# Attention with heads of 96 taken by pairs of tiles instead of by heads, with shared key chunks, and the last linear layer put inside it for one half of the rows

## The chip, the cores and the metric

The kernel runs on one core of one Trainium2 chip. The metric is the device time of one execution in microseconds (us); before the change the median of three runs is 1843.64 us (1840.32 to 1844.16). Six names are used for what works in a core: PE is the tensor engine (matrix products; "PEld" its weight loads), DVE the vector engine, ACT the scalar engine, POOL the GpSimd engine, SP the engine whose queue issues the loads and stores (DMAs), and PSUM the memory of eight banks into which PE writes.

## The reference

Four decoder layers, each a cross-attention and a feed-forward step, on 16 sequences of 64 tokens with width 512. Everything is float32. The change concerns the last layer, and moves some memory of the third. What matters of it, shortened:

```python
# layer 3, attention: 16 query heads, 4 key/value heads, head width 96
hidden = concatenate([context, latents], axis=1)          # 64 + 64 rows per sequence
q = (latents @ Wq.T).reshape(b, 64, 16, 96)
k = (hidden @ Wk.T).reshape(b, 128, 4, 96)
v = (hidden @ Wv.T).reshape(b, 128, 4, 96)
scores = einsum('bkgqd,bksd->bkgqs', q, k) / sqrt(96)     # 4 query heads share a key head
out = einsum('bkgqs,bksd->bkgqd', softmax(scores), v)
x = x + out.reshape(b, 64, 16 * 96) @ Wo.T
# layer 3, feed-forward: a 3-bit weight, unpacked in groups of 32
w = weight_q3 / 7.0 * (x_max - x_min) + x_min
x = x + layernorm(x) @ w.T + bias
```

Each step works on the layernorm of x, and adds to x.

## The kernel before, in words

**Tiles.** The 1024 rows are eight tiles of 128 rows (two sequences each); x lies in on-chip memory as `x[0]` to `x[7]`. `kvT` holds, transposed, the normed rows and the context rows of every tile.

**Lanes.** Two streams of work share the engines, lane a (`main`) and lane b (`side`). Lane b does the first layer, lane a the attention of the second; then lane b does layers 1f, 2 and 3 for tiles 0 to 3 and lane a the same for tiles 4 to 7. Each lane has four PSUM banks of its own (`Lane.bank`, tag `ps_a` or `ps_b`, `bufs=4`).

**Order.** Each layer is a generator that yields a planner's cost after each step, and `merged` runs lane b's steps until their costs have caught up with lane a's. PE executes in exactly the order in which these steps are written out (`manual_schedule` names PE alone). The other engines and the SP queue get an order from a planner that lays out the instructions when their inputs are ready. `ticks(units, steps)` (L184) is a software pipeline: in tick n, each step of the list, in order, works on unit n minus its lag.

**Slots.** A tile taken from a pool with a tag gets one of that tag's `bufs` pieces of memory, and keeps it until its last reader is done; the next tile of the tag waits for a free one. This holds for PSUM banks too.

**`packed_attention`** (L1153) first computes the values of the eight sequences of the lane (`v_all`, L1177), while `Normed.need` keeps the layernorms and their transposes (`xn`, an own tag with two slots) a little ahead. Then its units run head by head: (head h, tile pair t), eight per lane. Per unit: `keys` (L1209; four chunks of the contraction, 96 outputs wide, 512 columns), `scores` of the unit before, `queries` (L1224; three output chunks of 128, 256 columns each, in two banks), `turn_weights` (transposes of the softmaxed p, L137), `project` (L590), `values` (L581). `Attention.weights` makes p: two tiles p per unit (one per tile), both with tag `p` and `bufs=2`. Its exponentials (L556) read the scores' bank and write p, so that a bank of scores stays taken until its p has a slot. A head's weights are loaded once per lane, two heads ahead of need at most.

**Two instructions per product.** The program writes one float32 product of 128 rows; the profile counts two instructions for it. 128 of L1209 are thus 2 lanes x 2 pairs x 4 heads x 4 chunks, doubled. A transposition is one instruction.

**`q3_ffn`** (L1282) runs after the attention: it unpacks the weight in four parts on DVE (L1315, L1318, L1319), transposes them (L137, `wf`), and for each tile does layernorm, a transposition and the product (L1344), and stores the tile (L1348). Lane b ends first; lane a then runs alone to the end.

**Memory of weights.** The four `page`s of a lane (8 KB per partition each) serve layers 1f to 3 and are never given back.

Of the kernel before, what the change touches and what calls it, by code (L numbers as in the profile page):

```python
# [17 lines left out]
P = 128  # L18
# [125 lines left out]
class Normed:  # L144
# [3 lines left out]
    def __init__(self, ln, pool, tiles):  # L148
        self.ln, self.pool, self.tiles = ln, pool, tiles
        self.n_norm = self.n_tr = 0  # L150
        self.xn = {}

    def norm(self, t):
        xn = self.pool.tile([P, D], F32, tag="xn", name="xn", bufs=2)
        self.ln.layernorm(t, xn)
        self.xn[t] = xn
# [27 lines left out]
def ticks(units, steps, gate=lambda unit: None):  # L184


    for n in range(len(units) + max(lag for lag, _, _ in steps)):
        if n < len(units):
            need = gate(units[n])
            if need is not None:  # L190
                yield need
        for lag, step, cost in steps:
            if 0 <= n - lag < len(units):
                step(units[n - lag])
                yield cost
# [330 lines left out]
class Attention:  # L526


    G = 4
# [367 lines left out]
def small_head_attention(ln, tiles, w_in):  # L897
# [15 lines left out]
    with ExitStack() as es:  # L913
# [6 lines left out]
        normed = Normed(ln, pool, tiles)  # L920
# [232 lines left out]
def packed_attention(ln, tiles, w_in, w_v):  # L1153
# [5 lines left out]
    with ExitStack() as es:  # L1159
        pool = ln.pool(es, "l3a")  # L1160
# [4 lines left out]
        wv = ln.page("l3a_wv", NC * NKV * HD)  # L1165
        nc.sync.dma_start(wv, w_v)
        wv = wv.rearrange("p (c n) -> p c n", c=NC)
        normed = Normed(ln, pool, tiles)
        normed.need(-1)
        nb = 2 * len(tiles)  # L1170
        v_all = pool.tile([P, nb, NKV * HD], F32, tag="v_all", name="v_all", bufs=1)
        for i, t in enumerate(tiles):
            normed.need(i)
            for j in range(2):
                ps = ln.bank([P, NKV * HD], "ps_v")
                for c in range(NC):
                    nc.tensor.matmul(  # L1177
                        ps,
                        lhsT=k.both(c, 2 * t + j),
                        rhs=wv[:, c, :],  # L1180
                        start=c == 0,
                        stop=c == NC - 1,
                    )
                nc.scalar.copy(v_all[:, 2 * i + j, :], ps)
                yield 2.6
        heads, kept = {}, {}

        def head_weights(h):
            if h < NKV and h not in heads:
                n_q, n_k = NC * G * HD, NC * HD  # L1190
                n = n_q + n_k
                wa, wb = ln.page(f"l3a_w{h}", n), ln.page(f"l3a_o{h}", NJ * D)
                nc.sync.dma_start(wa, w_in[h, :, :n])
                nc.sync.dma_start(wb, w_in[h, :, n:])
                heads[h] = (
                    wa[:, :n_q].rearrange("p (c n) -> p c n", c=NC),
                    wa[:, n_q:n].rearrange("p (c n) -> p c n", c=NC),
                    wb.rearrange("p (g n) -> p g n", g=NJ),
                )

        def keys(u):
            h, t = u
            if t == tiles[0]:
                head_weights(h)
                head_weights(h + 1)
            wk = heads[h][1]
            ps = ln.bank([HD, 4, P], "ps_k")
            for c in range(NC):
                nc.tensor.matmul(  # L1209
                    ps, lhsT=wk[:, c, :], rhs=k.kvT[:, c, t : t + 2], start=c == 0, stop=c == NC - 1  # L1210
                )
            kT = pool.tile([HD, 4, P], F32, tag="kT", name="kT")
            nc.scalar.copy(kT, ps)
            kept[u] = dict(kT=kT)

        def queries(u):
            h, t = u
            wq = heads[h][0]
# [18 lines left out]
            kept[u]["qT"] = qT  # L1237

        def scores(u):
            d = kept[u]  # L1240
            qT, kT = d.pop("qT"), d.pop("kT")
            d["p"] = [
                at.weights(qT[:, 2 * i : 2 * i + 2], [kT[:, 2 * i + j] for j in range(2)])
                for i in range(2)
            ]
# [5 lines left out]
        def values(u):  # L1251
            h, t = u
            d = kept[u]
            aP = pool.tile([P, NJ, 4, S], F32, tag="aP", name="aP")
            for i, pT in enumerate(d.pop("pT")):
                b = 2 * (tiles.index(t) + i)
                ps = at.values(pT, v_all[:, b : b + 2, h * HD : (h + 1) * HD])
# [8 lines left out]
        def project(u):  # L1266
            h, t = u
            aP = kept.pop(u)["aP"]
            for i in range(2):
# [4 lines left out]
                at.project(t + i, chunks, heads[h][2])  # L1274

        yield from ticks(
            [(h, t) for h in range(NKV) for t in tiles[::2]],
            [
                (0, keys, 3.4),
                (1, scores, 1.8),  # L1280
                (0, queries, 5.2),
                (2, turn_weights, 0.9),  # L1282
                (3, project, 5.2),
                (2, values, 1.7),
            ],
        )


def q3_ffn(ln, tiles, w_q, w_ranges, bias, out):

    k, nc = ln.k, ln.nc
    GRP = 32
    NGR = D // GRP
    q3 = ln.page("w_l3f", 2048).bitcast(I32)
    nc.sync.dma_start(q3, w_q)
    with ExitStack() as es:
        pool = ln.pool(es, "l3f")
        wf = pool.tile([P, NC * D], F32, tag="wf", name="wf", bufs=1)
        r16 = pool.tile([P, NC * NGR, 2], F16, tag="r16", name="r16", bufs=1)
        nc.sync.dma_start(r16, w_ranges)  # L1300
        b16 = pool.tile([P, D], F16, tag="b16", name="b16", bufs=1)
        nc.sync.dma_start(b16, bias.partition_broadcast(P))
        bf = pool.tile([P, D], F32, tag="bf", name="bf", bufs=1)
        nc.vector.tensor_copy(bf, b16)
        r = pool.tile([P, 2, NC * NGR], F32, tag="r", name="r", bufs=1)
        nc.vector.tensor_copy(r, r16.rearrange("p n j -> p j n"))
        nc.vector.tensor_tensor(r[:, 1, :], r[:, 1, :], r[:, 0, :], ALU.subtract)
        wT = pool.tile([P, NC, D], F32, tag="wT", name="wT", bufs=1)
        kept = {}

        def values(u):
            kind, i = u
            if kind == "w":
                part = wf[:, i * D : (i + 1) * D]
                nc.vector.tensor_scalar_mul(part, q3[:, i * D : (i + 1) * D], 1.0 / 7.0)  # L1315
                w3 = part.rearrange("p (n i) -> p n i", i=GRP)
                groups = slice(i * NGR, (i + 1) * NGR)
                nc.vector.tensor_tensor(w3, w3, bc(r[:, 1, groups], 2, GRP), ALU.mult)  # L1318
                nc.vector.tensor_tensor(w3, w3, bc(r[:, 0, groups], 2, GRP), ALU.add)  # L1319
                kept[u] = part  # L1320
            else:
                xn = pool.tile([P, D], F32, tag="xn", name="xn")
                ln.layernorm(i, xn)
                nc.gpsimd.tensor_tensor(k.x[i], k.x[i], bf, ALU.add)
                kept[u] = xn

        def turn(u):
            kind, i = u
            ps = ln.transposed(kept.pop(u), NC, "ps_xT")
            if kind == "w":  # L1330
                nc.scalar.copy(wT[:, :, i * P : (i + 1) * P], ps)
            else:
                xT = pool.tile([P, NC, P], F32, tag="xT", name="xT")
                nc.scalar.copy(xT, ps)
                kept[u] = xT

        def product(u):
            kind, i = u
            if kind == "w":
                return  # L1340
            xT = kept.pop(u)
            ps = ln.bank([P, D], "ps_o")
            for c in range(NC):
                nc.tensor.matmul(  # L1344
                    ps, lhsT=xT[:, c, :], rhs=wT[:, c, :], start=c == 0, stop=c == NC - 1
                )
            ln.add_to(i, ps)
            nc.sync.dma_start(out[i * P : (i + 1) * P, :], k.x[i])  # L1348

        units = [("w", i) for i in range(NC)] + [("x", t) for t in tiles]  # L1350
        yield from ticks(units, [(0, values, 2.0), (2, product, 3.4), (1, turn, 0.5)])
# [35 lines left out]
def decoder_kernel(ctx: ExitStack, tc: tile.TileContext, i: dict, out: bass.AP):  # L1387
# [37 lines left out]
    def last_layers(ln, tiles):  # L1425
        yield from small_head_attention(ln, tiles, i["l2a_w"])
        yield from lora_experts(ln, tiles, i["l2f_a"], i["l2f_r"], i["l2f_b"])
        yield from packed_attention(ln, tiles, i["l3a_w"], i["l3a_v"])
        yield from q3_ffn(ln, tiles, i["l3f_q"], i["l3f_r"], i["l3f_b"], out)

    def side():
        yield from first_layers(b)
        b.pages(ctx)
        yield from mxfp4_ffn(b, halves[0], i["l1f_w"], i["l1f_b"])
        yield MARK
        yield from last_layers(b, halves[0])

    def main():
# [4 lines left out]
        yield Need(len(groups) + 1, 1.0)  # L1443
        a.pages(ctx)
        yield from mxfp4_ffn(a, halves[1], i["l1f_w"], i["l1f_b"])
# [9 lines left out]
def laid_out(a):  # L1455
# [19 lines left out]

    def per_head(wq, wk, wv, wo, hd, n_kv):
        rows = []

        order = np.arange(4 * hd)
        if hd < P:  # L1480
            order = [
                np.r_[j * hd : (j + 1) * hd, 3 * hd + (P - hd) * j : 3 * hd + (P - hd) * (j + 1)]
                for j in range(3)
            ]
            order = np.concatenate(order)
        for h in range(n_kv):
# [3 lines left out]
            rows.append(np.concatenate([q, chunks(np.concatenate(kv, 1)), o], 1))  # L1490
# [18 lines left out]
    i["l3a_w"] = per_head(w[0], w[1], None, w[3], 96, 4)  # L1509
# [23 lines left out]
```

## Time and profile before

| what | value |
|---|---|
| median of three runs | 1843.64 us |
| the profiled execution, device time | 1843.46 us |
| its span on the core | 1841.7 us |
| PE busy | 1733.7 us, 94% of the span |
| DVE, ACT, POOL busy | 52%, 33%, 27% of the span |
| loads and stores, mean | 83 GB/s |
| lane a alone, 1700 to 1804 us: PE busy | 99.35 us of 104 |
| after the last projection, 1804 to 1841.7 us: PE busy | 22.87 us of 37.7 |

The span is what the profile shows, 1.8 us less than the device time of the same execution. PE's "busy" covers the whole latency of each product (592 ns for 128x512), though the next one starts before it has ended; so the cost of an instruction in a full stream is read from a run of them: twelve of L590 take 5.42 us, and the starts lie 0.43 us apart.

Groups of the page that the change touches:

| group | instructions | mean ns |
|---|---|---|
| L1209 keys, 128x512 | 128 | 592 |
| L1224 queries, 128x256 | 384 | 380 |
| L590 projection of this attention, 128x512 | 192 | 599 |
| L1344 last product, 128x512 | 64 | 636 |
| loads of a head's query and key weights / output weights | 8 / 8 of 960 / 768 KB | 5.0 / 4.2 us to landing |

### The profile page before, as it was taken

The page shows a single profiled execution, that of the slowest core. Times are in us where ns is not written, and L with a number is a line of the kernel's source. Part 1 is how long each engine was busy: PE and PEld are TensorE (multiplying, and loading weights), DVE is VectorE, ACT ScalarE, POOL GpSimd, SP SyncE. Part 2 cuts the span into 40 slices and gives each one's busy share as a digit, 9 for nine tenths or more (in the row PEclk, how much of TensorE's full clock was granted, in tenths as well). Part 3 has the DMA queues.
Part 4 walks back from the last instruction along what each step waited for, and adds up shares of the span by engine and source line. Part 5 has one row for each costly group of instructions (what it writes and reads, how often), then busy time and mean ns, then how long its engine had stood idle before and what let it go on. Part 6 is the DMA issues. An engine that isn't in the chain of part 4 may idle for free.

```text
span 1841.7 us, 21657 instructions
## 1 busy us (share of the span) xinstructions
PE 1733.7 (94%) x7660; PEld 984.5 (53%) x7660; DVE 960.7 (52%) x2048; ACT 614.4 (33%) x1933; POOL 504.5 (27%) x494
## 2 busy tenths in 40 slices
PE   7899999998999999998998999989999999999996
PEld 2324355565554665555655566545566565565653
DVE  5544476564665556565588426486245332342234
ACT  2212353243432344423343434321234222333341
POOL 1443225632146321364232203121022100111011
PEclk9889999998999999999999999999999999999998
DMA  9212222232131223231354223221110101111100
GB/s 288 78 55 75 86 76 101 89 117 82 66 123 66 101 94 130 82 108 66 124 188 144 94 86 111 86 73 39 62 62 18 48 18 62 43 39 40 39 24 26
DMA packets 62266, 152.19 MB, mean 83 GB/s; under 512 B 31696, under 2 KB 40784, under 8 KB 51280
## 3 DMA queue, kind: packets, MB, share of 16 engines
q1 hardware_dynamic: 62160, 150.83, 24.1%
q8 instruction: 61, 1.00, 0.2%
q14 instruction: 45, 0.37, 0.1%
HBM read 140.32 MB, written 10.49 MB: 82 GB/s over the span
## 4 chain that ended last, share of the span: by engine, by line
PE 60%; DVE 12%; POOL 6%; ACT 4%; DMA 1%; issue 1%; ACTq 0%; SPq 0%; POOLq 0%; DVEq 0%
PE ps_wo L590 12%; PE ps_q L720 6%; PE ps_q L1224 5%; PE ps_kv L738 3%; PE ps_a L581 3%; PE ps_s L541 3%; PE ps_h L1117 3%; PE ps_o L1142 3%; PE ps_k L1209 3%; PE ps_v L1177 2%; ACT p L556 2%; DVE pv L377 2%; PE ps_pT L137 2%; PE ps_o L1344 2%; POOL pv L378 2%; POOL r L119 2%
## 5 line engine op out<-in xcount | busy, mean ns | idle before, releaser
L720 PE MATMUL ps_q<-l1a_w,kvT 128*128 128x512 f32 x512 | 234.2, 601 | 0.0
L590 PE MATMUL ps_wo<-l1a_o,aT 128*128 128x512 f32 x512 | 233.0, 598 | 1.2 <-ACT aT L784 1.2
L556 ACT ACTIVATE p<-ps_s,mx 128x128 f32<-128x128 f32 x384 | 135.8, 368 | 265.8 <-DVE mx L552 183.0
L565 POOL TENSOR_TENSOR p<-p,sm 128x512 f32<-128x512 f32 x96 | 103.6, 1080 | 383.6 <-DVE sm L564 330.8
L119 POOL TENSOR_TENSOR r<-r,mhalf 128x5 f32<-128x5 f32 (+1 forms) x96 | 105.2, 1096 | 329.0 <-DVE r L667 316.3
L590 PEld LDWEIGHTS ps_wo<-l1a_o,aT 128*128 128x128 f32 x512 | 95.1, 191 | 121.2 <-issue 116.7
L141 DVE TENSOR_TENSOR x<-x,ps_wo 128x512 f32<-128x512 f32 x104 | 70.8, 680 | 165.0 <-PE ps_wo L590 145.3
L720 PEld LDWEIGHTS ps_q<-l1a_w,kvT 128*128 128x128 f32 x512 | 94.0, 193 | 100.3 <-issue 100.1
L738 PE MATMUL ps_kv<-l1a_w,kvT 128*128 128x256 f32 x512 | 128.3, 396 | 3.7 <-ACT qn L730 3.5
L677 PE MATMUL ps_ckv<-l1a_kv,kvT 128*64 128x512 f32 x512 | 125.0, 633 | 2.8 <-DMA l1a_kv<-in_l1a_kv 2.8
L666 DVE TENSOR_REDUCE r<-sq 128x5 f32<-128x640 f32 (+1 forms) x96 | 65.5, 682 | 118.4 <-ACT sq L746 60.4
L738 PEld LDWEIGHTS ps_kv<-l1a_w,kvT 128*128 128x128 f32 x512 | 96.4, 198 | 18.3 <-ACT qn L730 5.6
L541 PEld LDWEIGHTS ps_s<-kT,qT 128*128 128x128 f32 (+1 forms) x768 | 97.7, 193 | 11.4 <-issue 6.0
L119 POOL TENSOR_TENSOR rs<-rs,mhalf 128x1 f32<-128x1 f32 x64 | 37.7, 594 | 229.2 <-DVE rs L128 220.5
L541 PE MATMUL ps_s<-kT,qT 128*128 128x128 f32 (+1 forms) x768 | 100.2, 277 | 0.0
L137 PE MATMUL ps_pT<-ident,p 128*128 128x128 f32 x512 | 76.7, 281 | 21.2 <-DVE x L141 9.4
L754 DVE TENSOR_TENSOR qn<-qn,r 128x512 f32<-128x512 f32 x64 | 45.3, 708 | 96.5 <-POOL r L119 95.1
L378 POOL TENSOR_TENSOR pv<-pv 128x1024 f32<-128x1024 f32 x32 | 75.3, 2352 | 66.0 <-DVE pv L377 63.3
L551 DVE TENSOR_REDUCE mx<-ps_s 128x4 f32<-128x512 f32 x96 | 65.6, 684 | 49.5 <-PE ps_s L541 49.4
L293 DVE TENSOR_TENSOR prod<-qs,kp 128x1024 f32<-128x1024 f32 x64 | 80.6, 1288 | 20.1 <-ACT kp L269 16.6
L590 PE MATMUL ps_wo<-l3a_o,aP 128*128 128x512 f32 x192 | 86.3, 599 | 4.5 <-DVE pT L572 2.4
L137 PEld LDWEIGHTS ps_pT<-ident,p 128*128 128x128 f32 x512 | 61.4, 144 | 48.5 <-issue 37.8
(205 smaller groups left out, 2939.0 us busy)
## 6 DMA issues: line engine op xcount, KB each, us to landing
l1a_w<-in_l1a_w SPq DMA_DIRECT2D x32, 1536.0 KB, 6.9
l1a_o<-in_l1a_w SPq DMA_DIRECT2D x32, 1024.0 KB, 5.1
s<-ckv SPq DMA_DIRECT2D x32, 256.0 KB, 2.0
l3a_w<-in_l3a_w SPq DMA_DIRECT2D x8, 960.0 KB, 5.0
l3a_o<-in_l3a_w SPq DMA_DIRECT2D x8, 768.0 KB, 4.2
l1a_kv<-in_l1a_kv SPq DMA_DIRECT2D x4, 1024.0 KB, 5.6
kT<-s SPq DMA_DIRECT2D x64, 64.0 KB, 2.8
v<-s SPq DMA_DIRECT2D x128, 32.0 KB, 2.6
```

Of the source, the lines that this page charges most:

```text
L119: self.nc.gpsimd.tensor_tensor(out, v, self.k.mhalf[:, : v.shape[1]], ALU.pow)
L137: self.nc.tensor.transpose(ps[:, c, :], src[:, c * P : (c + 1) * P], ident)
L293: nc.vector.tensor_tensor(prod[:, w : w + 2, :], bc(qs, 1, 2), windows(kp, g * NG + w, 2, D), ALU.mult,)
L378: nc.gpsimd.tensor_tensor(pv[:, 0:2, :], pv[:, 0:2, :], pv[:, 2:4, :], ALU.add)
L541: nc.tensor.matmul(ps[:, i, :], lhsT=qT[:, i // 2, 2 * (i % 2) : 2 * (i % 2) + 2, :].rearrange("p g s -> p (g s)"), rhs=kTs[i // 2], start ...
L556: nc.scalar.activation(p[:, i, :], ps[:, i, :], AF.Exp, bias=mx[:, i : i + 1], scale=self.scale, accum_out=sm[:, i : i + 1],)
L565: nc.gpsimd.tensor_tensor(p, p, bc(sm, 2, P), ALU.mult)
L590: self.nc.tensor.matmul(ps, lhsT=a, rhs=wo[:, g, :], start=g == 0, stop=g == len(chunks) - 1)
L677: nc.tensor.matmul(ps[j * S : (j + 1) * S], lhsT=k.context(c, 2 * t + 1 - j), rhs=w_pair[hp][:, c, :], start=c == 0, stop=c == NC - 1,)
L720: nc.tensor.matmul(ps, lhsT=k.stream(c, t), rhs=w_qkv[n][0][:, c, :], start=c == 0, stop=c == NC - 1,)
L738: nc.tensor.matmul(ps, lhsT=k.stream(c, t), rhs=w_qkv[n][1][:, c, :], start=c == 0, stop=c == NC - 1,)
L1224: nc.tensor.matmul(ps[:, j], lhsT=wq[:, c, (j0 + j) * P : (j0 + j + 1) * P], rhs=k.kvT[:, c, t : t + 2, 1:3, :], start=c == 0, stop=c == N ...
```

## The change

- **Units by pairs of tiles.** The units of `packed_attention` are now (t, h): all four heads of one tile pair, then of the other. Before the first head of a pair, `context_side` computes the pair's values and the keys of all four heads.
- **Keys in full chunks.** The keys of four heads are 384 rows; they are computed as three chunks of 128 outputs instead of four of 96. The weight's columns are reordered on the host so that a chunk holds the 96 rows of one head and 32 of the fourth; two copies take a chunk apart. The step `keys` leaves the ticks.
- **Weights.** The pages end with `lora_experts`. A new pool `l3w` has two slots `q` (query weights of a head, and the shared value and key weights) and three slots `o` (output weights). Every pair loads all of them anew.
- **Layernorm tiles.** `Normed` takes a tag: in `packed_attention` its tiles now use the tag `p`, in `small_head_attention` the tag `aT`, in place of `xn`.
- **The last layer in between.** `q3_ffn` becomes a class. In lane a its steps join the attention's ticks: the weight's parts are unpacked and transposed during the second pair's heads, the first pair's two tiles are normed, turned and multiplied during the second pair, and the last two tiles after the last projection. Lane b runs it after its attention as before, with two slots `row` for the four unpacked parts (which had a place each).
- A mark that made lane a wait for lane b's layer 1f goes.

```diff
-        xn = self.pool.tile([P, D], F32, tag="xn", name="xn", bufs=2)
+        xn = self.pool.tile([P, D], F32, tag=self.tag, name="xn", bufs=2)
...
+            if units[n] in before:
+                yield from before[units[n]](units[n][0])
...
-        normed = Normed(ln, pool, tiles)
+        normed = Normed(ln, pool, tiles, "p")
         normed.need(-1)
...
+                two = [
+                    wpool.tile([P, n], F32, tag="q", name="l3a_wq"),
+                    wpool.tile([P, NJ * D], F32, tag="o", name="l3a_wo", bufs=3),
+                ]
...
+        def context_side(t0):
+            shared = []
+            for w in (w_v, w_k):
+                page = wpool.tile([P, NC * NKV * HD], F32, tag="q", name="l3a_wkv")
+                nc.sync.dma_start(page, w)
...
+            if t0 == pairs[-1] and ffn is not None:
+                ffn.open(es)
+            for t in (t0, t0 + 1):
+                normed.need(tiles.index(t))
...
+            head_weights((t0, 0))
+            kTs = [pool.tile([HD, 4, P], F32, tag="kT", name="kT", bufs=6) for _ in range(NKV)]
+            for j in range(NJ):
+                ps = ln.bank([P, 4, P], "ps_k")
...
+                nc.scalar.copy(kTs[j], ps[:HD])
+                nc.scalar.copy(kTs[NJ][R * j : R * (j + 1)], ps[HD:])
+                yield 3.4
...
         def queries(u):
-            h, t = u
-            wq = heads[h][0]
+            t, h = u
+            head_weights(u)
+            if h + 1 < NKV:
+                head_weights((t, h + 1))
+            wq = heads[u][0]
...
-                (0, keys, 3.4),
...
+        steps = [
+            (1, scores, 1.8),
+            (0, queries, 5.2),
+            (2, turn_weights, 0.9),
+            (3, project, 5.2),
+            (2, values, 1.7),
+        ]
+        if ffn is not None:
...
+            steps += [
+                (1, of_weights(ffn.turn_weights), 0.4),
+                (0, of_weights(ffn.weights), 0.0),
+                (5, after(ffn.product), 0.2),
+                (3, after(ffn.norm), 0.0),
+                (4, after(ffn.turn), 0.2),
+            ]
+        units = [(t, h) for t in pairs for h in range(NKV)]
+        yield from ticks(units, steps, before={(t, 0): context_side for t in pairs})
...
+    def weights(self, i):
+        nc, r = self.ln.nc, self.r
+        part = self.pool.tile([P, D], F32, tag="row", name="wf")
...
+        with ExitStack() as es:
+            ln.pages(es)
+            yield from mxfp4_ffn(ln, tiles, i["l1f_w"], i["l1f_b"])
+            yield from small_head_attention(ln, tiles, i["l2a_w"])
+            yield from lora_experts(ln, tiles, i["l2f_a"], i["l2f_r"], i["l2f_b"])
+        ffn = Q3Ffn(ln, i["l3f_q"], i["l3f_r"], i["l3f_b"], out)
+        last = ln is a
+        yield from packed_attention(
+            ln, tiles, i["l3a_w"], i["l3a_k"], i["l3a_v"], ffn if last else None
+        )
+        if not last:
+            yield from ffn.run(tiles)
```

`Normed.need(i)`, which the change leaves as it is, norms up to tile i+2 of the lane and transposes up to tile i+1:

```python
while self.n_norm < min(i + 3, n) or self.n_tr < min(i + 2, n):
    if self.n_norm < n and self.n_norm < self.n_tr + 2:
        self.norm(self.tiles[self.n_norm])
        self.n_norm += 1
    else:
        self.turn(self.tiles[self.n_tr])
        self.n_tr += 1
```

## The prediction

> **What bounds the kernel now.** First the page's head and its slices.
>
> ```profile
> span 1841.7 us, 21657 instructions
> PE 1733.7 (94%) x7660; PEld 984.5 (53%) x7660; DVE 960.7 (52%) x2048; ACT 614.4 (33%) x1933; POOL 504.5 (27%) x494
> PE   7899999998999999998998999989999999999996
> PEclk9889999998999999999999999999999999999998
> ```
>
> PE is busy in every slice but the first and the last, and it takes its steps in a written order. So a product that goes is worth its place in PE's stream, and a wait of PE costs its whole length. Next the chain of waits at the end, where lane a is alone.
>
> ```profile
> 1804.75 1.34 DVE wf L1315 x4
> ...
> 1808.22 2.82 DVE wf L1318 x2
> ...
> 1814.10 2.84 PE ps_xT L137 x12
> ...
> 1817.60 5.67 PE ps_o L1344 x8
> ...
> 1834.12 3.71 PE ps_o L1344 x8
> ```
>
> The last projection ends at 1804.0. Then DVE unpacks the last layer's weight while PE stands for 7.8 us; the first eight L1344 take 5.67 us where later eights take 3.70. Last, one tick of lane a's attention in the timeline (start, length, engine, line):
>
> ```profile
> 1765.82 5.35 PE L1224 MATMUL ps_q<-kvT,l3a_w 128*128 128x256 f32 x24
> 1769.48 0.69 DVE L1231 COPY qT<-ps_q 96x512 f32<-96x512 f32 x1 [2.56 <-PE ps_q L1224]
> 1770.25 0.75 ACT L1236 COPY qT<-ps_q 32x256 f32<-32x256 f32 x2 [5.44 <-DVE qT L1231]
> 1771.10 0.63 PE L137 MATMUL ps_pT<-ident,p 128*128 128x128 f32 x4
> ...
> 1771.82 0.37 ACT L556 ACTIVATE p<-ps_s,mx 128x128 f32<-128x128 f32 x1 [0.82 <-PE ps_pT L137]
> ...
> 1772.60 0.63 PE L137 MATMUL ps_pT<-ident,p 128*128 128x128 f32 x4 [0.87 <-DVE pT L572]
> ```
>
> The next unit's scores were ready at 1766, but its first exponential starts at 1771.82, released by the transposes of the older p. So the two slots of tag p limit the softmax already; a whole tick hides it.
>
> **1. Keys in full chunks.** 64 products become 2 lanes x 2 pairs x 3 chunks x 4 = 48, so 128 instructions become 96. Eight L1209 in lane a alone hold PE for 3.43 us (1701.43 to the scores at 1704.86): 0.43 each. 32 x 0.43 = **-13.7 us**. Query and projection counts stay. A key chunk now needs two ACT copies, some 1.2 us (0.58 today) beside 3.4 us of PE; with ACT busy 39 of 104 us in lane a's stretch I cost them at nothing.
>
> **2. The end of lane a.** Today 37.7 us from the last projection to the end of the span. After the change only two tiles remain. Around 1794.33 the trace shows add, statistics and POOL's power ending in 3.2 us at the earliest moment for the normed tile. So, from the end of the projection: second tile normed 3.3; its transposes to 4.0; two products of 8 x 0.43 to 10.9; then from the last add to the end 3.8 (1837.92 to 1841.7), sum 14.8. The gap may cost half a microsecond of clock: 15.3. That is -22.4. What moves into PE's stream counts: 24 transposes (eight took 1.04) 3.1 us, 16 L1344 6.9 us. Net **-12.4 us**. The unpacking rides on DVE, busy 35 of 104 us there; if it came late, the 7.8 us of today would stand inside.
>
> **3. Layernorm tiles in the slots of p.** `Normed.need` runs ahead. At the first pair, `need(0)` and `need(1)` norm all four tiles of the lane but transpose only three; the fourth is transposed by `need(2)`, when the second pair begins. Until then it sits in one of p's two slots. Each unit has two p, so for two units of each lane (those turned before the second pair begins) the second p must wait until the first is transposed, and its transposes come next in PE's order, with no step between. Nothing can cover that: behind them PE holds projections and values of both lanes.
> - Price of the wait, from the tick above: exponentials start 0.72 after the first transposes start; from 1784.23 to 1787.23 the next tick's timeline has exponentials, reciprocal and POOL's multiply in 3.0 us; 0.1 to PE. The second transposes start 3.8 us after the first, an idle of 3.3. Today they wait 0.9 in lane a and nothing where lanes are mixed. Ends: 0 and 3.8 each; I take 3.3 twice (lane b), 2.4 twice (lane a): +11.4.
> - The late p also keeps its scores in a PSUM bank. With the next unit's two banks, three of four are taken, and `queries` needs two in turn: its second group waits for the first's copies, to 1771.0, where 16 of its 24 instructions ended at 1769.3: 1.8 us. Ends 0 and 2.5; four times 1.8 = +7.2, and 0.7 once where no step of lane b stands before the transposes.
> - The clock. The nearest row is an earlier wait of PE between transposes:
>
> ```profile
> 595.76 0.60 PE L137 MATMUL ps_qT<-ident,qn 128*128 128x128 f32 x4
> 599.85 0.47 PE L137 MATMUL ps_kT<-ident,kn 128*128 128x128 f32 x1 [3.49 <-ACT p L556]
> 600.81 3.78 PE L738 MATMUL ps_kv<-l1a_w,kvT 128*128 128x256 f32 x8 [0.49 <-ACT qn L730]
> ```
>
> and that stretch in the windows view (length, PE busy, granted clock, DMA):
>
> ```profile
> 599.60:606.40 6.80, 6.07 (x16) 0.50 0.14 28
> ```
>
>  Eight L738 take 3.78 us where at 1005.9 they take 1.89. Busy 6.07 us at half clock loses 3.0; the same happens after 841.94 (3.1), and a wait of 1.57 at 564.14 loses 1.6 of 3.3 us. The Trainium skill, "TensorE: Matmul & The Clock Gate", Part 1, says that an idle window of about 3.4 us halves the clock; read so, a wait of 3.3 us would mostly escape: 0. Its Part 4 (PE-mode transpose) adds that transposes do not count as busy; then each of our waits is 3.3 + 1.2 of transposes + about 1 before, and falls. The rows side with the second. By the rule 4 x one window at half = 6.8; by the three rows' mean, 2.5 each, 10.0. I take **10.0** (ends 0 and 13.6, two windows each).
>
> Sum of part 3: 11.4 + 7.2 + 0.7 + 10.0 = **+29.3 us**.
>
> **4. Lane b's last layer with two `row` slots.** Parts three and four now wait for transposes of parts one and two. In PE's order parts two, three and four are transposed back to back; the fourth's unpacking (L1315, L1318, L1319: 0.35, 0.64, 0.64) can start only when the second is turned, 0.55 before: **+1.4** including semaphores. Ends 0 and 3.3.
>
> **5. At nothing, with the cover.** Loads: 18 become 40 (2 lanes x 2 pairs x 2 shared and 8 of heads), 768 KB in 4.0 to 4.2 us. A pair's first query weights reuse the slot of the value weights and have 24 key instructions, 10.2 us, to land; later heads have transposes, projection, values, scores, 10 us. Without cover 4.3 each, four times, 17. Output weights have three slots and wait for the projection of three units before; if SP had one of them ahead of the second pair's value weights, those would come 2 to 3 us late per lane. SP waits in order (one load stood 39 us behind L581 near the end), but its planner places loads by readiness; I take 0. The new pools lie where pages and layer 2 lay; the first value weights can at worst leave after the last L1142, with lane b's transposes, projection and values (8 us) against 4.0 of landing. Steps that leave the ticks: scores now follow values directly, and queries were copied out 8 us before. The mark changes nothing: lane b has passed it when lane a asks (the planner's costs, added by hand).
>
> **Sum.** -13.7 - 12.4 + 29.3 + 1.4 = +4.6. Against its own execution, 1841.7 of span and 1.8 around it, 1843.5; that gives **1848 us**. The median of the runs shown is 1843.64, so the two bases agree.
>
> **Rivals.**
> - **The clock stays up** (ends on the other side). Place: the four waits of part 3; price: 10.0 us. If the slower windows do not come, or fall into the waits, the sum is -5.4: 1838. The sign turns where they cost less than 1.4 us each. For: two of the four waits stand in mixed lanes where small products precede; against: three rows of three fell. If even the waits did not arise, because the fourth tile's slot were free by then, 1843.5 - 26.1 + 1.4 = 1819; the exponentials of today, released by transposes, speak against it.
> - **Half of them fall**: 1843, no change.
> - **The waits are longer.** ACT and POOL take their work in order too: in the two lane-b waits lane a's small heads want POOL (1.04 us each) and ACT (0.6), and lane b's additions of the bias (L1324, 1.3) stand beside lane a's. With 1.5 more in each and some loads late: 1856.
> - **Only the end gains** if the keys' place in the stream was covering something: 1843.5 + 4.6 + 7 at most, 1855. Against: lane a alone has PE busy 99.35 of 104 us, with no such wait.
>
> **Chances.** Forecast (1845 to 1853) 0.38; clock up 0.21; waits absent 0.08; half 0.20; longer waits and late keys 0.13. The range 1833 to 1858 leaves out the absent waits and the far tail, under 0.2. Of a bound of 0.2%, 3.7 us, which is what a measurement of this kernel can tell: faster 0.30, within 0.26, slower 0.44; the cases at the bound are split. As signs are mixed, the likeliest one's own range is 1845 to 1853.
>
> **What would show it.** L1209 with 96 instructions; the span's end some 15 us after the last projection, with 16 L1344 in it. Part 3: in two ticks of each lane L137 waits some 3 us for POOL's p (L565), L1224 waits for ACT's qT, and the granted clock falls to half behind. If p's exponentials run in pairs there as today, part 3 is wrong and the time is near 1819. PE waiting for loads of l3a weights would make part 5 wrong.

## The result, and the profile after

The changed kernel takes 1860.05 us, median of six runs (1856.77 to 1865.44); the kernel before took 1843.9 in the same series. The ratio is 1.0098, 95% interval 1.0083 to 1.0114: slower by about 18 us (16 between the two medians). The forecast was slower by 4.6 us, to 1848, with a range that ended at 1858. The direction was right, the size was not.

The page's head and slices of the changed kernel:

```profile
span 1854.7 us, 21638 instructions
...
PE 1725.2 (93%) x7628; PEld 984.2 (53%) x7628; DVE 960.7 (52%) x2048; ACT 619.9 (33%) x1941; POOL 504.6 (27%) x494
...
PE   7899999998998999998999999989988899997998
...
PEclk9889999998998999999999999999999999998999
```

PE is busy 8.5 us less than before, while the span is 13 us longer: work has gone and waits have come. The profiled execution is the fastest of the six (1856.77 us), and it was 5.4 us ahead of the profiled one of before when the changed part began: the last keys of layer 2's small heads (L929, before L926) start at 1299.1 us, before at 1304.5, after the same PE steps in the same order. From there to the end it takes 555.6 us for 537.2, which is 18.4 us more. The slices show where: three slices of 8 in a row, from about 1345 to 1484 us (a slice is 46.4 us), and one of 7 from 1669 us on, where before PE had 9 throughout; the last slice, 6 before, is now 8.

The waits of PE from 1300 us to the end (who waits, for whom, total, times, longest):

```profile
PE ps_pT L137 <- POOL p L568: 13.6, 4, 3.8
PE ps_q L1245 <- ACT qT L1257: 6.5, 4, 1.8
...
PE ps_r L1088 <- DMA wr<-in_l2f_r: 3.6, 1, 3.6
PE ps_pT L137 <- ACT qT L1257: 2.0, 3, 1.0
PE ps_pT L137 <- DVE p L1000: 1.9, 1, 1.9
PE ps_xT L137 <- DVE wf L1368: 1.9, 1, 1.9
PE ps_v L1206 <- ACT kvT L160: 1.8, 2, 1.5
PE ps_s L986 <- DVE sm L1004: 1.7, 1, 1.7
```

The first two lines did not exist before: four waits for POOL's p and four for the queries' copies. They are the slot that the fourth tile keeps. In this part of the kernel the line of 3.6 us for a load and that of L986, the scores of the small heads, are new too, and the prediction did not have them. One of the four ticks, in PE's timeline, and then two stretches in the windows view (length, PE busy, granted clock):

```profile
1367.31 3.98 PE L1245 MATMUL ps_q<-kvT,l3a_wq 128*128 128x256 f32 x16
1373.11 1.99 PE L1245 MATMUL ps_q<-kvT,l3a_wq 128*128 128x256 f32 x8 [1.82 <-ACT qT L1257]
...
1376.70 0.63 PE L137 MATMUL ps_pT<-ident,p 128*128 128x128 f32 x4 [0.72 <-ACT qT L1257]
1381.15 0.66 PE L137 MATMUL ps_pT<-ident,p 128*128 128x128 f32 x4 [3.83 <-POOL p L568]
1381.64 3.58 PE L584 MATMUL ps_a<-pT,v 128*96 128x256 f32 x8
```

```profile
1381.60:1385.00 3.40, 3.40 (x10) 0.51 0.00 0
...
1474.60:1480.90 6.30, 6.26 (x14) 0.52 0.00 0
```

The queries' last eight instructions wait 1.82 us for a bank; the second transposes wait 3.83 us; the eight value products behind them take 3.58 us at a clock of 0.51, where eight take 1.89 at full clock (at 1413.06). The second stretch follows the wait for the load.

The end of the chain of waits:

```profile
1832.63 2.85 PE ps_wo L593 x6
...
1838.55 0.61 DVE x L141
...
1842.26 8.58 PE ps_o L1393 x16
...
1850.93 0.69 DVE x L141
```

From the end of the last projection (1838.1) to the end of the span 16.6 us pass, where it was 37.7. DVE takes the last tile's addition only behind the tile before it. The sixteen product instructions of the last two tiles take 8.58 us where sixteen took 6.87 at 1818: PE had stood 0.6 and 2.3 us between their transposes, and the granted clock from 1842.5 to 1846 is 0.52.

### The profile page after: what moved, and what is told of

Same layout as the page of the kernel before. It is cut to its first block, busy times and chain, and to the rows that moved or that the text cites. A ratio compares the mean times of both kernels' runs of the same rounds, so it can differ in the third digit from the quotient of the medians.

```text
span 1854.7 us, 21638 instructions
## 1 busy us (share of the span) xinstructions
PE 1725.2 (93%) x7628; PEld 984.2 (53%) x7628; DVE 960.7 (52%) x2048; ACT 619.9 (33%) x1941; POOL 504.6 (27%) x494
## 4 chain that ended last, share of the span: by engine, by line
PE 59%; DVE 12%; POOL 6%; ACT 5%; DMA 2%; issue 1%; ACTq 0%; SPq 0%; POOLq 0%; DVEq 0%
PE ps_wo L593 12%; PE ps_q L723 6%; PE ps_q L1245 4%; PE ps_kv L741 4%; PE ps_s L544 3%; PE ps_a L584 3%; PE ps_h L1120 3%; PE ps_o L1145 3%; PE ps_k L1221 2%; ACT p L559 2%; PE ps_v L1206 2%; PE ps_pT L137 2%; DVE pv L380 2%; PE ps_o L1393 2%; PE ps_q L968 1%; POOL r L119 1%
## 5 line engine op out<-in xcount | busy, mean ns | idle before, releaser
L137 PE MATMUL ps_pT<-ident,p 128*128 128x128 f32 x512 | 77.3, 280 | 36.0 <-POOL p L568 13.6
L544 PEld LDWEIGHTS ps_s<-kT,qT 128*128 128x128 f32 (+1 forms) x768 | 100.4, 198 | 10.3 <-issue 4.2
L544 PE MATMUL ps_s<-kT,qT 128*128 128x128 f32 (+1 forms) x768 | 103.9, 283 | 0.1
L584 PE MATMUL ps_a<-pT,v 128*128 128x256 f32 (+1 forms) x384 | 99.2, 389 | 0.1
L137 PEld LDWEIGHTS ps_pT<-ident,p 128*128 128x128 f32 x512 | 60.8, 144 | 65.1 <-issue 39.9
L1245 PE MATMUL ps_q<-kvT,l3a_wq 128*128 128x256 f32 x384 | 87.0, 381 | 6.5 <-ACT qT L1257 6.5
L593 PE MATMUL ps_wo<-l3a_wo,aP 128*128 128x512 f32 x192 | 90.1, 621 | 2.2 <-DVE pT L575 1.5
```

The costliest lines, as they stand in the source:

```text
L137: self.nc.tensor.transpose(ps[:, c, :], src[:, c * P : (c + 1) * P], ident)
L544: nc.tensor.matmul(ps[:, i, :], lhsT=qT[:, i // 2, 2 * (i % 2) : 2 * (i % 2) + 2, :].rearrange("p g s -> p (g s)"), rhs=kTs[i // 2], start ...
L584: self.nc.tensor.matmul(ps[:, j, :, :], lhsT=v[:, j, :], rhs=pT[:, j, :], start=True, stop=True)
L593: self.nc.tensor.matmul(ps, lhsT=a, rhs=wo[:, g, :], start=g == 0, stop=g == len(chunks) - 1)
L1245: nc.tensor.matmul(ps[:, j], lhsT=wq[:, c, (j0 + j) * P : (j0 + j + 1) * P], rhs=k.kvT[:, c, t : t + 2, 1:3, :], start=c == 0, stop=c == N ...
```

## The experiments

Times of different groups come from different chips (the kernel before has medians of 1839.96 to 1841.25 in them), so ratios to the kernel before are compared; a ratio's interval reaches 0.09 to 0.24% to either side, 2 to 4 us, and a difference of two ratios is uncertain by some 3 to 5 us. The theory on trial, the **slot theory**: the fourth tile in p's slot makes most of the loss. The rival, the **order theory**: the loss comes of what stands beside what in the mixed lanes (what the key steps covered, and the loads), and the waits for p are one place of several where it shows.

**The fourth tile transposed where the third was** (and the third one step earlier), so that it is out of its slot before the first scores:

```diff
-                normed.need(tiles.index(t))
+                normed.need(tiles.index(t) + 1)
```

> The fourth tile of each lane is transposed with the third, before the first pair's heads, so that it leaves its slot of p in time; the same work, four transposes earlier in PE's order. Slot theory: the four waits of L137 for POOL's p (13.6 us in the changed kernel's trace, about 0.9 of it ordinary in each of lane a's two), the waits of L1245 for qT (6.6) and of L137 for qT (2.0) go, and four slow-clock stretches behind them (about 8): some 28 us less than the changed kernel, 1832 us, below the kernel before. Order theory (what the key steps covered in the mixed lanes, and the loads): these waits were a symptom, others take their place; not more than 5 us less, 1855 us or above.

Measured: 1827.41 us, ratio 0.9929 (0.9913 to 0.9946). The edit is worth 1.69%, 31 us, and turns the change from a loss into a gain. The waits for POOL's p and L1245's for qT are gone, as the slot theory said, and six times what the order theory allowed is gained. At the top of what is left from 1300 us on, two lines are ordinary; the load and the small heads stay:

```profile
PE ps_xT L137 <- DVE xn L130: 5.4, 6, 2.3
PE ps_pT L137 <- DVE pT L575: 5.2, 6, 0.9
PE ps_r L1088 <- DMA wr<-in_l2f_r: 3.1, 1, 3.1
PE ps_s L986 <- DVE sm L1004: 2.2, 1, 2.2
```

**The router's weight loaded before the pages:**

```diff
     wa, wb = [], []
-    for ws, src in ((wa, w_a), (wb, w_b)):
...
         pool = ln.pool(es, "l2f")
         wr = pool.tile([P, NC, KE], F32, tag="wr", name="wr", bufs=1)
         nc.sync.dma_start(wr.rearrange("p c n -> p (c n)"), w_r)
+        for ws, src in ((wa, w_a), (wb, w_b)):
```

> In lora_experts the small load wr is issued before the four pages instead of behind them; nothing else. In the changed kernel lane a's first router product waits 3.6 us for wr, which left only when the page of w_l2o was free, and the clock is halved behind it. Slot theory: this is a small part, 5 to 7 us less than the changed kernel, 1853 to 1855 us. Order theory: more than half of the 16 us lost, 8 us or more less, 1852 us or below. If wr's own memory comes free only with layer 2's last products, no change, 1860.

Measured: 1847.95 us, ratio 1.0044 (1.0029 to 1.0059): 9.9 us less than the changed kernel, more than the slot theory gave (5 to 7); here the order theory's number (8 or more) came. The wait goes in both lanes. Part of this was to be had before the change too, where lane b waits 2.7 us for the same load:

**The same edit in the kernel before.**

> The kernel before, with wr issued before the pages. There only lane b waits for wr (2.7 us at 1228, clock halved behind it); lane a has 6 us of other work between. So 3 to 5 us less than the kernel before, ratio 0.998; if the 10 us that this edit took off the changed kernel were there before too, 0.9945.

Measured: 1835.71 us, ratio 0.9971 (0.9959 to 0.9983), 5.3 us. So some 4.6 us of the 9.9 belong to the change, with an uncertainty as large as themselves. The traces place them: from the small heads' last keys to the end, the early load brings the changed kernel from 555.6 us to 546.4, and the kernel before from 537.2 to 536.3 (one execution each). Lane a's wait belongs to the change; lane b's, further ahead, is in both kernels. The changed kernel's SP queue (start, length, what it issues) shows how the load came late:

```profile
1434.17 31.41 SPq L1182 DMA_DIRECT2D l3a_wq<-in_l3a_w  x3
1468.68 0.33 SPq L1073 DMA_DIRECT2D w_l2f<-in_l2f_b  x1
1469.11 0.37 SPq L1079 DMA_DIRECT2D wr<-in_l2f_r  x1
```

The small load stands behind that of a page, and the page comes free with the small heads' last projection, at 1468.6. Before, transposes and a projection of lane b stood between that projection and the router, 1453.2 to 1460.0 in PE's timeline; in the changed order lane b's steps fall otherwise, and the router comes next (both timelines stand in part 5 below).

**Both edits.**

> Both edits together. If they are independent the gains add: 28 and 6 us, 1826 us, about 0.990 of the kernel before. If the second wait was only uncovered by the first, the sum is smaller: 1832.

Measured: 1820.91 us, ratio 0.9898 (0.9884 to 0.9913). The two add to within their intervals: 0.0169 and 0.0054 alone (0.0223), 0.0200 together.

**The early transposition in lane b alone** (`tiles.index(t) + (1 if tiles[0] == 0 else 0)`).

> The fourth tile is transposed early in lane b alone; lane a keeps it in p's slot as in the changed kernel. Slot theory: half of the waits go (3.8 + 3.5 for POOL's p, 3.4 for qT, 0.7) and two slow-clock stretches; the ratio to the kernel before lies half way between the changed kernel's 1.0098 and 0.9929 of the run with both lanes, 1.001. If one lane's wait only moved the stall to the other lane, near 1.009.

Measured: 1842.27 us, ratio 1.0001 (0.9989 to 1.0014). Half the cure gives half the gain, within the interval of 1.001. The stalls don't move to the other lane. The order theory, which called the waits a symptom, falls as the main cause; it keeps the part of the load.

**Real products in the gap.** Does a wait cost only its length?

```diff
         def turn_weights(u):
             d = kept[u]
-            d["pT"] = [at.turned(p) for p in d.pop("p")]
+            two = d.pop("p")
+            d["pT"] = [at.turned(two[0])]
+            if u[0] == pairs[0] and u[1] < 2:
+                ps = ln.bank([P, 4, P], "ps_fill")
+                for c in range(3):
+                    nc.tensor.matmul(ps, lhsT=k.both(c, 2 * u[0]), rhs=k.kvT[:, c, u[0] : u[0] + 2],
+                                     start=c == 0, stop=c == 2)
+            d["pT"].append(at.turned(two[1]))
```

> The changed kernel, and between the transposes of the first and the second p of the four late units three extra products of kvT with itself (six instructions, 2.6 us of PE), into a bank that nobody reads. They fit into the wait of 3.1 to 3.8 us, so PE's order has no longer to stand there, and the second transposes start at most 0.3 us later. Clock theory: what the wait costs beyond its length is the halved clock behind it, some 8 us for the four; it stays up with real products in the gap, so about 7 us less than the changed kernel, ratio 1.006. If the halved clock is worth little, or comes of other waits, the same or a little more: 1.010.

Measured: 1852.62 us, ratio 1.0062 (1.0045 to 1.0079), 6.6 us less by doing 24 instructions more. In PE's timeline of this run, two of the four gaps:

```profile
1383.08 2.84 PE L1275 MATMUL ps_fill<-kvT 128*128 128x512 f32 x6 [0.78 <-DVE pT L575]
1386.12 0.66 PE L137 MATMUL ps_pT<-ident,p 128*128 128x128 f32 x4 [0.20 <-POOL p L568]
1386.61 2.05 PE L584 MATMUL ps_a<-pT,v 128*96 128x256 f32 x8
...
1405.89 5.19 PE L1275 MATMUL ps_fill<-kvT 128*128 128x512 f32 x6 [1.66 <-ACT p L559]
1410.91 0.60 PE L137 MATMUL ps_pT<-ident,p 128*128 128x128 f32 x4
```

In the first the value products now take 2.05 us, where the changed kernel shows 3.58. In the second the filler itself fell to half clock, since transposes and two waits of 1.9 and 1.7 us stood ahead of it; so 6.6 us is less than the whole of the clock's part. In the other two gaps the filler and the products behind it ran at full clock: of the four slow stretches one is left.

**The last layer after the attention in lane a too** (`last = False`), on the changed kernel.

> The changed kernel, but in lane a too the last linear layer runs after the attention, as in lane b. This gives back the end's gain, predicted as 12.4 us; the trace of the changed kernel has 16.6 us after the last projection instead of 37.7 and 10 us moved inside, so 11 to 12 us more than the changed kernel: 1871 to 1872 us. If putting it inside was hidden or paid elsewhere, near 1860.

Measured: 1869.64 us, ratio 1.0160 (1.0136 to 1.0184), 11.4 us more. From the end of the last projection (1826.8) to the end of the span 37.3 us pass, near the 37.7 of the kernel before. Its waits from 1700 us on begin with the unpacking that stood open before:

```profile
PE ps_xT L137 <- DVE wf L1368: 7.7, 4, 4.6
```

**Keys of 96, on top of both edits** (and the weight's columns in their own order again).

```diff
-            for j in range(NJ):
-                ps = ln.bank([P, 4, P], "ps_k")
+            for j in range(NKV):
+                ps = ln.bank([HD, 4, P], "ps_k")
...
-                        lhsT=wk[:, c, j * P : (j + 1) * P],
+                        lhsT=wk[:, c, j * HD : (j + 1) * HD],
...
-                nc.scalar.copy(kTs[j], ps[:HD])
-                nc.scalar.copy(kTs[NJ][R * j : R * (j + 1)], ps[HD:])
+                nc.scalar.copy(kTs[j], ps)
```

> Early fourth tile and early wr, but the keys computed in four chunks of 96 outputs instead of three of 128 (32 instructions more). Stream theory: each holds PE for 0.43 us, 13.7 us more than the run with both edits (ratio 0.9898): 0.9973 of the kernel before. If the three chunks' second copy or other waits hid the saving, under 7 us, below 0.9937.

Measured: 1836.4 us, ratio 0.9974 (0.9964 to 0.9983), 14.0 us more than with full chunks.

**Four slots `row` in lane b**, on top of both edits (`bufs=4` there for `row`).

> Early fourth tile and early wr, and in lane b four slots row instead of two, so that the last layer's four unpacked parts need not wait for each other's transposes. The wait of L137 for wf (1.9 us) goes, with perhaps one window of slow clock: 2 to 3.5 us less than the run with both edits, ratio 0.988 to 0.989. If DVE then does this work later than needed, 0.990.

Measured: 1818.85 us, ratio 0.9874 (0.9859 to 0.9888), 4.4 us less than with two slots; the two intervals overlap at their ends. It is the fastest version of the study, some 23 us below the kernel before.

**More of lane b before the small heads' second scores**, on top of that (`yield 3.2 if n == 0 and ln.name == "a" else 2.4`).

> The run with early fourth tile, early wr and four slots row, and in lane a the planner's cost of the small heads' first four softmax steps is raised from 2.4 to 3.2, so that one more tick of lane b (scores and queries, 7 us) stands before their second scores (L986), which wait 2.6 us and are followed by a window of slow clock. Order theory: this wait was covered by the key steps that the change took out of the ticks; 3 to 4.5 us less, ratio 0.985 to 0.986. If another wait takes its place, 0.987.

A miss: 1826.27 us, ratio 0.9921 (0.9909 to 0.9934), 8.7 us worse. L986's wait has gone, and these lines stand in its place:

```profile
PE ps_wo L593 <- DVE pT L575: 3.8, 7, 0.8
PE ps_s L544 <- ACT qT L1257: 3.5, 2, 2.3
...
PE ps_s L544 <- DVE qT L1252: 1.7, 1, 1.7
```

The cost moved all the steps behind it, and scores then followed their queries too closely: 5.2 us of waits for qT, 1.0 in the run without it. Slow clock stands behind both places (0.51 from 1363.7, 0.50 from 1633.4): the 24 queries there take 6.29 and 6.79 us, where they take 5.35. The rest of the 8.7 us was not traced. So the wait of L986 was not shown to cost what its line says.

## Why the prediction was right or wrong, point by point

In us. "By runs" is a difference of ratios times 1841, each uncertain by some 3 to 5. "In the trace" is read from the changed kernel's profiled execution, waits and half of the busy time at half clock added, against the 18.4 us that it takes longer from the small heads' last keys on.

| step of the prediction | predicted | by runs | from | in the trace |
|---|---|---|---|---|
| 1 keys in full chunks | -13.7 | -14.0 | keys of 96 against both edits | -13.7 |
| 2 the end of lane a | -12.4 | -11.4 | last layer after the attention | -11.1 |
| 3 the slot of p | +29.3 | +31.1 | early fourth tile | +28.7 |
| 4 two slots row | +1.4 | +4.4 | four slots | +3.6 |
| 5 the router's load | 0 | +4.6 | early load, less its gain before | +6.7 |
| 5 the small heads' scores | 0 | | no run shows it alone | +3.8 |
| what is left | | +3.3 | | +0.4 |
| sum | +4.6 | +18.0 | the changed kernel | +18.4 |

With both edits taken together (0.0200) in place of the two alone, what is left by runs is 7.5 and not 3.3; the runs alone do not settle the last rows.

**1 and 2 were right**, by their working. The end took 16.6 us and not 15.3: 1.7 for the slow clock and not 0.5, and DVE's order. (Its parts in the prediction add to 14.7, not 14.8.) That 1 to 3 come out within 2 us by runs is closer than those runs can tell.

**3 was right in mechanism and in size.** Its parts in the trace: waits for p 3.8, 3.5, 3.1 and 3.1 (3.3 predicted; 0.9 of each in lane a was there before), for the bank 1.8 and three times 1.6 (1.8), before the first transposes 0.7 and 1.0 (0.7 once). The clock behind the four waits: stretches with 3.4, 4.8, 3.5 and 5.65 us of busy PE at half clock, half of which is 8.7 us, for 10.0. The three older rows, not the bare length of an idle window, gave the right price. That all four fell was likely, not certain: of the fourteen such waits in the four profiled executions that have them, two of 3.1 us (at 1673.83 with the early load, at 1709.11 with the last layer after the attention) are followed by full clock. The rival "the clock stays up", 1838, is refuted by these stretches and by the 6.6 us of the filler.

**4 was mis-sized, by less than the runs can tell.** The wait was 1.9 us for 1.4 (L137 for wf), and the prediction let it end there. In the changed kernel's trace slow clock follows it:

```profile
1650.74 0.66 PE L137 MATMUL ps_xT<-ident,wf 128*128 128x128 f32 x4 [1.87 <-DVE wf L1368]
1651.23 3.52 PE L544 MATMUL ps_s<-kT,qT 96*128 96x128 f32 x16
```

Sixteen L544 otherwise take 1.95 us. The price that part 3 paid was not asked of this wait. But the same wait of 1.87 us with both edits, the kernel on which four slots were tried, is followed by 1.95; so of the 4.4 us by runs, 1.9 are seen and the rest is within the scatter.

**5 is the step that failed**: "At nothing, with the cover". It asked for every load of layer 3 what covers it, and those are in fact covered: no wait of PE for an l3a weight appears. It also said that the mark changes nothing, and PE's order is the same in both kernels until lane b's first keys, 1326 us. But it put the new order itself at nothing ("Steps that leave the ticks"), and looked only at what follows the attention's own steps. What changed is what stands between two steps of lane a. The router, before and after:

```profile
1446.27 7.13 PE L1033 MATMUL ps_wo<-w_l2o,aT 128*128 128x512 f32 x16
1453.24 1.04 PE L137 MATMUL ps_pT<-ident,p 128*128 128x128 f32 x8
1454.78 5.42 PE L590 MATMUL ps_wo<-l3a_o,aP 128*128 128x512 f32 x12 [0.51 <-DVE pT L572]
1460.04 1.04 PE L137 MATMUL ps_xT<-ident,xn 128*128 128x128 f32 x8
1461.31 1.10 PE L1085 MATMUL ps_r<-wr,kvT 128*128 128x64 f32 x8 [0.24 <-ACT kvT L160]
```

```profile
1465.05 3.60 PE L1036 MATMUL ps_wo<-w_l2o,aT 128*128 128x512 f32 x8
1469.98 1.08 PE L137 MATMUL ps_xT<-ident,xn 128*128 128x128 f32 x8 [1.33 <-DVE xn L130]
1474.64 1.94 PE L1088 MATMUL ps_r<-wr,kvT 128*128 128x64 f32 x8 [3.57 <-DMA wr<-in_l2f_r]
```

The load lost its cover of 6.4 us (transposes and a projection) and cost a wait of 3.6 us and half of a slow stretch with 6.3 us of busy PE: 6.7 in the trace, 4.6 by runs. The small heads' second scores, before and after:

```profile
1357.09 5.45 PE L1224 MATMUL ps_q<-kvT,l3a_w 128*128 128x256 f32 x24
1362.38 3.60 PE L1209 MATMUL ps_k<-kvT,l3a_w 128*96 128x512 f32 x8
1365.90 1.21 PE L983 MATMUL ps_s<-kbd,qT 32*64 32x128 f32 x64
```

```profile
1361.00 0.43 PE L986 MATMUL ps_s<-kbd,qT 32*64 32x128 f32 x4 [0.37 <-DVE p L1000]
1363.12 1.09 PE L986 MATMUL ps_s<-kbd,qT 32*64 32x128 f32 x52 [1.69 <-DVE sm L1004]
1364.14 3.38 PE L544 MATMUL ps_s<-kT,qT 96*128 96x128 f32 x16
```

They had 8.8 us of lane b ahead of them (queries and keys) and now 7.2 (scores and queries, from 1353.02); they wait 2.1 us in two pieces, and the stretch behind, 3.5 us of busy PE at a clock of 0.52, costs 1.7 more. This is read from the trace, not shown by a run: the one that was to show it (a higher cost in lane a) opened other waits. Together the two places make 10.5 of the 13.8 us by which the trace exceeds the forecast; part 4 makes 2.2. Which part of the change re-dealt the order, the keys' leaving the ticks or the units by pairs, no run separates.

The chances were set on the right side (slower 0.44), but the range was cut at 1858. The rival of "longer waits" at 1856 named POOL and ACT; what came was other waits. Nearest in kind was "Only the end gains", 1855, which asked whether the keys' place in the stream was covering something, but looked for it in lane a alone; the cover that was lost stood where the lanes are mixed.

## What to carry to other kernels

When two kinds of tile share a tag, ask when the last reader of each comes in the order of the engine that reads it: one tile that outlives a phase takes away half of a double buffer, silently, and transposing it one place earlier gave 31 us back. When the order of an engine is dealt out by costs, a step taken out in one stream changes the cover of every step in the other; list the pairs that now stand next to each other, loads included. Price every new wait of PE with the slow clock behind it, also the short ones, as a chance: the same wait can pay it in one run and not in the next.

## What the runs showed of the hardware

Short waits among transposes and small products can be followed by half clock, and the same wait isn't always. The wait of 1.87 us for wf, between eight and four transposes, is followed by half clock in two of the seven profiled executions that have it (the changed kernel, from 1651.3, and the run with the last layer after the attention) and by full clock in the other five. The waits of 0.4 and 1.7 us among the small products L986 are followed by half clock from 1364.5. The four waits of 3.1 to 3.8 us for p all are in the changed kernel, twelve of fourteen in all runs that have them. The Trainium skill, "TensorE: Matmul & The Clock Gate", Part 4, says that transposes do not count as busy in the same way as products; these rows fit that, though no run here tests it alone.

Real products put into a gap made the kernel 6.6 us faster: 24 extra instructions cost less than the clock that they kept.
